# A four-layer graph network on one core: edge lists laid on 128 partitions instead of 125, and two products split into 12-bit parts

## The chip, the core and the metric

The program runs on one core of a Trainium2 chip. The core has five engines that follow their own instruction streams and wait for each other by semaphores: TensorE (PE, with its weight loads shown as PEld), VectorE (DVE), ScalarE (ACT), GpSimd (POOL) and SyncE (SP). SP, ACT and POOL also issue DMAs, each from its own queue, and all DMAs are carried out by 16 DMA engines. The metric is the device time of the whole program in microseconds; smaller is better.

## The reference

There are 3125 nodes with 256 features and 53125 directed edges (25000 random ones, their reverses, and one loop per node), sorted by target node. Four layers follow each other; each adds its result to `x`.

```python
h = relu(layernorm(x))
# layer 0: message network
m   = relu(concat(h[src], h[dst], edge_attr) @ eW1 + eb1) @ eW2 + eb2
agg = segment_sum(m, dst)
x  += layernorm(h + mlp(concat(h, agg)))
# layer 1: attention over incoming edges, with a 64-entry table of relations
k   = K[src] + 0.2 * rel_w[edge_type]        # 4 heads of 64
w   = softmax over the edges of dst of (Q[dst] . k) / 8
x  += layernorm(segment_sum(w * V[src]) @ Wo + bo + h)
# layer 2: attention with one softmax over ALL edges, edges grouped by source
# layer 3: attention with self loops, then the gates of an LSTM cell
```

## The kernel before

Nodes are handled in 25 blocks of 128. The program has a `prelude`, which counts and sorts, and then `by_slots`, which does the four layers. If a flag that the prelude computes is 0, another path (`by_blocks`) runs in its place; on these inputs the flag is 1 as long as every source block's edge count lies within the bounds that the prelude checks.

**Prelude.** The list of edges is read as `EP, EC = 125, 425`: 125 partitions with 425 consecutive edges each. `dst_i` comes by SP's queue (L254), `e_src`, `e_typ` and the shifted list `nxt_i` by ACT's queue (L261, L263, L267). After `dst_i`, SP's queue carries `x` (four loads of 6 blocks at L257 and one of the last 53 nodes at L259), the weights `w1a`, the one-row bias `b1`, and 40 DMAs that fill the whole record table `ss` with a default record (L305). DVE compares the edges with 128 low and 25 high node numbers (L330, L332; `ol` and `oh` have one buffer each, so the second half of the columns waits until PE has used the first), PE sums products of these into the degrees `pdeg` (L334). PE's stream starts with two products of `b1` (L361) that stand ahead of the first `pdeg`. Between the halves stand layer norms of `x` and the first rows of the table `a_d` of layer 0's source values. From the degrees come ranks, a scatter of the nodes in order of degree, and gathers of each node's edges into slots (`t.st`). From running sums over source blocks comes `row2`, the row of `ss` that each edge's record goes to.

**The scatter of records.** Layer 2 needs the edges grouped by source. So during layers 0 and 1 each column of the edge list is scattered to `ss`: `scatter_src(1)` issues one indirect DMA on POOL (`Kit.scatter`, L158) with one record of 66 floats from each partition, 425 in all. The records stand in `rec` tiles of `CH = 5` columns, two buffers; `loaded` reads 64 edge features per record by SP's queue (L588), one chunk ahead, and `filled` writes the two index columns by two DVE copies (L592, L593).

**Layer 0.** Work goes over 226 pairs of slots. For each pair POOL issues two gathers of 512 values (`gt`, ring of 5 pairs), and from the 19th pair on one record scatter. PE forms `ph` by two products of 128 rows (L924): the stationary operand `st` holds on one half of its rows the transposed edge features and on the other half an identity, the moving operand `wm` holds on the one half the edge rows of `eW1` and on the other half the block's own node values. DVE adds `gt` (L938) and sums the positive parts into `acc` (L941, L943). A `Clock` with ticks places the other work of a block between the pairs: `front` (node values into `wm`, two ACT copies at L715), `turned` (features into `st`, two ACT copies of 64 partitions at L733, L734), `back`, `group` and `node`. When the pairs are done, ticks go on until the last nodes are through, one record scatter at each tick; the last scatters of `kv` rows (`s_l_kv`) stand behind these on POOL, and layer 1's gathers behind them.

**Layer 1.** For each unit of up to 4 slots SP loads the slots' relation numbers, broadcast over 64 partitions (`tb`, two buffers, L980), ACT makes a one-hot of it (L985, L986), PE multiplies it by the relations (L990), POOL gathers `kv` rows (ring of 10 units), DVE forms scores (L992 on). `weighed` takes the softmax of a finished block while the next one is scored; it frees the `kv` buffers by DVE products and PE sums (L1032). `nodes` makes the rows for layer 2 (`s_l_rows`). The remaining record scatters are spread evenly over the units; the last 8 come at the end.

**Layers 2 and 3** are not touched.

The order of instructions on each engine's queue is made by a scheduler at build time, which places an instruction where its own model finds it ready. It is not the order of the source text.

Of the kernel before, what the change touches and what calls it, by code (L numbers as in the profile page):

```python
# [18 lines left out]
P = 128  # L19
# [31 lines left out]
assert sum(TILES) == NT  # L51
XH = 516
# [171 lines left out]
class Lists:  # L224


    def __init__(self, pool):
# [9 lines left out]
        self.row2 = pool.tile([EP, EC], I32, name="row2")  # L237
        self.dst_e = pool.tile([EP, EC], F32, name="dst_e")
        self.srcl_e = pool.tile([EP, EC], F32, name="srcl_e")
# [3 lines left out]
def prelude(ctx, tc, a, a_d, nodes_d, ss, st_d, flag, t):  # L243
# [9 lines left out]
    dst_i = c.tile([EP, EC], I32, name="dst_i")  # L253
    nc.sync.dma_start(dst_i, a["dst"].rearrange("(p c) -> p c", c=EC))  # L254
# [5 lines left out]
    e_src = c.tile([EP, EC], I32, name="e_src")  # L260
    nc.scalar.dma_start(e_src, a["src"].rearrange("(p c) -> p c", c=EC))  # L261
    e_typ = c.tile([EP, EC], I32, name="e_typ")
    nc.scalar.dma_start(e_typ, a["edge_type_64"].rearrange("(p c) -> p c", c=EC))  # L263
    nxt_i = c.tile([EP, EC], I32, name="nxt_i")
    nc.gpsimd.memset(nxt_i, N)
    for p0, p1, w in ((0, EP - 1, EC), (EP - 1, EP, EC - 1)):
        nc.scalar.dma_start(nxt_i[p0:p1, 0:w],  # L267
                            bass.AP(tensor=a["dst"].tensor, offset=a["dst"].offset + p0 * EC + 1,
                                    ap=[[EC, p1 - p0], [1, w]]))
# [6 lines left out]
    sfill = c.tile([P, 11, SREC], F32, name="sfill")  # L276
# [12 lines left out]
    nc.gpsimd.memset(cap[:, NB - 1:NB], float(P * TILES[NB - 1]))  # L289
    none = c.tile([1, 512], F32, name="none")  # L290
# [13 lines left out]
    for i in range(40):  # L304
        nc.sync.dma_start(ss[i * 11 * P:(i + 1) * 11 * P, :].rearrange("(p r) c -> p (r c)", p=P),  # L305
                          sfill.rearrange("p r c -> p (r c)"))

    both_e = c.tile([EP, EC, 2], I32, name="both_e")
    nc.gpsimd.tensor_copy(both_e[:, :, 0], e_src)
    nc.gpsimd.tensor_copy(both_e[:, :, 1], e_typ)  # L310
    nc.scalar.dma_start(st_d.rearrange("(p c) -> p c", c=2 * EC), both_e.rearrange("p c i -> p (c i)"))


    lo_i = wk.tile([EP, EC], I32, name="lo_i", tag="edge", bufs=4)
    nc.vector.tensor_scalar(lo_i, dst_i, 127, None, op0=ALU.bitwise_and)
    lo = c.tile([EP, EC], BF, name="lo")
    nc.vector.tensor_copy(lo, lo_i)
    hi_i = wk.tile([EP, EC], I32, name="hi_i", tag="edge", bufs=4)
    nc.vector.tensor_scalar(hi_i, dst_i, 7, None, op0=ALU.logical_shift_right)
    hi = c.tile([EP, EC], BF, name="hi")  # L320
    nc.vector.tensor_copy(hi, hi_i)
    pdeg = ps.tile([P, NB], F32, name="pdeg")
    CW = 214

    def counted(hp, c0, c1):
        w = c1 - c0
        ol = hp.tile([EP, P, CW], BF, name="ol")
        oh = hp.tile([EP, NB, CW], BF, name="oh")
        for v in range(P):
            nc.vector.tensor_scalar(ol[:, v, 0:w], lo[:, c0:c1], float(v), None, op0=ALU.is_equal)  # L330
        for v in range(NB):
            nc.vector.tensor_scalar(oh[:, v, 0:w], hi[:, c0:c1], float(v), None, op0=ALU.is_equal)  # L332
        for i in range(w):
            nc.tensor.matmul(pdeg, ol[:, :, i], oh[:, :, i], start=(c0 + i == 0), stop=(c0 + i == EC - 1))  # L334
# [33 lines left out]
    with tc.tile_pool(name="ph", bufs=1) as hp:  # L368
        counted(hp, 0, CW)
        stats()  # L370
        table(0, 5)
        counted(hp, CW, EC)
# [73 lines left out]
    sl_i = wk.tile([EP, EC], I32, name="sl_i", tag="edge", bufs=4)  # L446
    nc.vector.tensor_scalar(sl_i, e_src, 127, None, op0=ALU.bitwise_and)
    nc.vector.tensor_copy(t.srcl_e, sl_i)
    hs_i = wk.tile([EP, EC], I32, name="hs_i", tag="edge", bufs=4)
    nc.vector.tensor_scalar(hs_i, e_src, 7, None, op0=ALU.logical_shift_right)  # L450
    hs = c.tile([EP, EC], BF, name="hs")
    nc.vector.tensor_copy(hs, hs_i)
    eq = op.tile([EP, NB, EC], BF, name="eq")
# [3 lines left out]
    zero = ps.tile([EP, EC], F32, name="zero")  # L457
    nc.vector.memset(zero, 0.0)
    cum = op.tile([EP, NB, EC], F32, name="cum")
# [8 lines left out]
    tots = c.tile([EP, NB], F32, name="tots")  # L468
    nc.vector.tensor_copy(tots, cum[:, :, EC - 1])
    pc3 = ps.tile([P, 4, NB], F32, name="pc3")  # L470
    pc2, pv = pc3[:, 0:2, :], pc3[0:1, 2, :]
    nc.tensor.matmul(pc2[:EP, 0, :], k.tri[:EP, :EP], tots, start=True, stop=True)
    nc.tensor.matmul(pc2[:, 1, :], k.ones[:EP, :], tots, start=True, stop=True)
    viol = wk.tile([EP, EC], F32, name="viol", tag="edge", bufs=4)
    nc.vector.tensor_tensor(viol, dst_i, nxt_i, ALU.is_gt)
    v1 = c.tile([EP, 1], F32, name="v1")
# [5 lines left out]
    nc.vector.tensor_tensor(over, pc2[:, 1, :], cap, ALU.is_gt)  # L482
    v3 = c.tile([P, 1], F32, name="v3")
    nc.vector.tensor_reduce(v3, over, AX.X, ALU.add)
    nc.tensor.matmul(pv[:, 0:1], v1, k.ones[:EP, 0:1], start=True, stop=False)
# [5 lines left out]
    bases = c.tile([EP, NB], F32, name="bases")  # L491
    nc.vector.tensor_scalar(bases, pc2[:EP, 0, :], -1.0, None, op0=ALU.add)
# [4 lines left out]
    for b in range(NB - 1, -1, -1):  # L497
        k.gather(t.st[:, b, 0:SLOTS[b], :].rearrange("p s i -> p (s i)"), flat(st_d, 2 * E), t.off_i[:, b:b + 1], axis=1)
# [46 lines left out]
    pos_i = wk.tile([EP, EC], I32, name="pos_i", tag="edge", bufs=4)  # L545
    nc.vector.tensor_copy(pos_i, cum[:, 0])
    pa_i = wk.tile([EP, EC], I32, name="pa_i", tag="edge", bufs=4)
    nc.vector.tensor_scalar(pa_i, pos_i, 127, None, op0=ALU.bitwise_and)
    pj_i = wk.tile([EP, EC], I32, name="pj_i", tag="edge", bufs=4)
    nc.vector.tensor_scalar(pj_i, pos_i, 7, None, op0=ALU.logical_shift_right)  # L550
    step = wk.tile([EP, EC], F32, name="step", tag="edge", bufs=4)
# [3 lines left out]
    nc.vector.scalar_tensor_tensor(t.row2, hs, float(P * TM), step, op0=ALU.mult, op1=ALU.add)  # L555
    nc.vector.tensor_scalar(t.dst_e, dst_i, float(KVQ), None, op0=ALU.mult)
# [3 lines left out]
def by_slots(ctx, tc, a, out, a_d, nodes_d, ss, t):  # L560
# [19 lines left out]
    attr = a["edge_attr_64"].rearrange("(p c) k -> p c k", c=EC)  # L580
    CH = 5
    recs = ctx.enter_context(tc.tile_pool(name="s_recs", bufs=2))
    done = [0]

    def loaded(c):

        rec = recs.tile([EP, CH, SREC], F32, name="rec")
        nc.sync.dma_start(rec[:, :, 0:64], attr[:, c:c + CH, :])  # L588
        return rec

    def filled(c, rec):
        nc.vector.tensor_copy(rec[:, :, 64], dst_e[:, c:c + CH])  # L592
        nc.vector.tensor_copy(rec[:, :, 65], srcl_e[:, c:c + CH])  # L593

    rec_of = {}

    def scatter_src(n):

        for _ in range(n):
            c = done[0]  # L600
            if c == EC:
                return
            c0 = c - c % CH
            if c == 0:
                rec_of[0] = loaded(0)
                filled(0, rec_of[0])
            if c % CH == 1 and c0 + CH < EC:
                rec_of[c0 + CH] = loaded(c0 + CH)
            if c % CH == 3 and c0 + CH < EC:
                filled(c0 + CH, rec_of[c0 + CH])  # L610
            k.scatter(ss, row2[:, c:c + 1], rec_of[c0][:, c % CH, :], "src_records")
# [5 lines left out]
    with tc.tile_pool(name="s_e0", bufs=2) as wk, tc.tile_pool(name="s_e0w", bufs=1) as w, \  # L617
# [4 lines left out]
        wm = [[w.tile([P, 512], F32, name=f"wm{i}{r}") for r in range(ring)] for i in range(2)]  # L622
        st = [[w.tile([P, 4, P], F32, name=f"st{i}{r}") for r in range(ring)] for i in range(2)]
        for i in range(2):
            lo = 64 * i
            at_ = 64 - lo
            for r in range(ring):
                nc.sync.dma_start(wm[i][r][at_:at_ + 64, :], a["L0_gnn_eW1"][2 * D:2 * D + 64, :])
                for q in range(4):
                    for h in range(2):  # L630
                        nc.scalar.copy(st[i][r][lo:lo + 64, q, h * 64:h * 64 + 64],
                                       ident[lo:lo + 64, lo:lo + 64])
        both = w.tile([P, 64], F32, name="both")
        for h in range(2):
            nc.scalar.copy(both[64 * h:64 * h + 64, :], ident[64 * h:64 * h + 64, 64 * h:64 * h + 64])
        w2 = k.load_w(w, a["L0_gnn_eW2"], "w2")
# [50 lines left out]
        def front(b):  # L687
# [24 lines left out]
            yield 1  # L712
            ms[b] = [wm[h][place[b] % ring] for h in range(2)]
# [1672 lines left out]
```

## Time and profile before

| what | value |
|---|---|
| median of 15 runs | 3773.26 us (3767.17 to 3785.41) |
| profiled execution, its own time | 3777.45 us |
| span of the profile | 3775.3 us |
| busy: PE, DVE, ACT, POOL | 2346.1, 2380.1, 1096.8, 2483.4 us |
| record scatters on POOL | 425, 513.4 us busy, 1208 ns mean |
| prelude | 0 to 235 us |
| layer 0, pairs | 235 to 1254 us |
| layer 0, last nodes | 1254 to 1386 us |
| layer 1 | 1386 to 2345 us |
| layer 2 | 2345 to 3060 us |
| layer 3 | 3060 to 3776 us |

The stages are read from the first and last instructions of their tiles. A line of the profile names an engine, a source line, an operation, the tiles out<-in, partitions x elements, and a count. "Idle before <- X" is the time in which the engine stood still ahead of that instruction, and what ended it; "issue" is a gap for which the profile shows no cause.

### The profile page before, as it was taken

To read this page: it belongs to the slowest core of one execution; us is meant where nothing else is said; L and a number is where in the kernel's file an instruction comes from. 1 tells how busy PE (TensorE), PEld (TensorE's weight loads), DVE (VectorE), ACT (ScalarE), POOL (GpSimd) and SP (SyncE) were. 2 spreads that over 40 slices of the span, in tenths; PEclk is the share of its full clock that TensorE was granted. 3 is DMA by queue.
4 is the path that set the end of the run, shared out by engine and by line. 5 is a ranking of instruction groups with operands and counts; after the bars stand their busy time and mean duration, and the time that the engine had idled before them with its cause. 6 is when DMAs were issued, how large, how long until landed. Compare 5 with 4: busy or idle time off the path is not lost. (4 is left out here: it accounts for less than half of the span.)

```text
span 3775.3 us, 32562 instructions
## 1 busy us (share of the span) xinstructions
PE 2346.1 (62%) x9174; PEld 1474.8 (39%) x9174; DVE 2380.1 (63%) x4836; ACT 1096.8 (29%) x2296; POOL 2483.4 (66%) x2497
## 2 busy tenths in 40 slices
PE   5827878788877654556656665898988950112223
PEld 3313434344343334445444543566666640001111
DVE  5646566576666326667767765798988953444444
ACT  1112122222221112122322221566666630112222
POOL 3447677777777736767767654676766617667774
PEclk9858889998898756667767767899999975555556
DMA  6346465666665346656666654666666623333342
GB/s 225 128 123 175 134 182 162 171 174 172 182 169 172 83 128 169 173 162 192 188 173 193 172 155 157 199 202 204 203 208 196 192 93 106 100 97 106 109 112 71
DMA packets 295839, 595.89 MB, mean 158 GB/s; under 512 B 113501, under 2 KB 154508, under 8 KB 295650
## 3 DMA queue, kind: packets, MB, share of 16 engines
q0 software_dynamic: 163616, 472.86, 43.3%
q1 hardware_dynamic: 131512, 119.79, 10.7%
q8 instruction: 76, 1.25, 0.1%
q10 hardware_dynamic: 522, 1.06, 0.1%
q14 instruction: 113, 0.93, 0.1%
HBM read 510.85 MB, written 82.21 MB: 157 GB/s over the span
## 5 line engine op out<-in xcount | busy, mean ns | idle before, releaser
L158 POOL DMA_INDIRECT s_src_records<-rec,row x425 | 513.4, 1208 | 131.2 <-issue 119.7
L154 POOL DMA_INDIRECT kv<-s_l_rows,dst x440 | 456.3, 1037 | 217.9 <-issue 75.6
L924 PE MATMUL ph<-wm,st 128*128 128x512 f32 x904 | 474.2, 653 | 130.9 <-DVE acc L943 65.3
L154 POOL DMA_INDIRECT gt<-s_l_src,srcb x452 | 433.9, 960 | 178.1 <-issue 108.2
L154 POOL DMA_INDIRECT kv<-s_l_kv,st x439 | 420.6, 958 | 182.0 <-issue 109.2
L154 POOL DMA_INDIRECT xg<-s_l_rows,src x439 | 416.2, 948 | 133.7 <-issue 133.4
L990 PE MATMUL pk<-rel,toh 64*128 64x64 f32 x878 | 179.0, 364 | 309.1 <-DVE mk L992 179.1
L938 DVE TENSOR_TENSOR ph<-gt,ph 128x1024 f32<-128x1024 f32 x226 | 277.1, 1226 | 110.7 <-PE ph L924 98.9
L134 PE MATMUL pt<-ident,hb 128*128 128x128 f32 x50 | 16.9, 441 | 513.3 <-ACT hb L1436 513.3
L924 PEld LDWEIGHTS ph<-wm,st 128*128 128x128 f32 x904 | 178.4, 208 | 334.1 <-issue 292.3
L990 PEld LDWEIGHTS pk<-rel,toh 64*128 64x128 f32 x878 | 159.8, 268 | 342.7 <-issue 245.7
L1032 PE MATMUL acc<-kv,ident 128*128 128x256 f32 x878 | 241.0, 442 | 41.5 <-DVE kv L1028 41.5
L592 DVE COPY rec<-dst_e 125x5 f32<-125x5 f32 x85 | 17.5, 205 | 380.2 <-DMA s_src_records<-rec,row 350.7
L1287 PE MATMUL pg<-kv,oh 128*128 128x256 f32 x880 | 249.8, 409 | 3.7 <-DVE kv L1284 3.4
L985 ACT ACTIVATE toh<-tb,negp 64x512 f32<-64x512 f32 (+3 forms) x119 | 81.8, 687 | 576.2 <-PE pk L990 496.7
L943 DVE SCALAR_TENSOR_TENSOR acc<-ph,acc 128x1024 f32<-128x1024 f32 x201 | 245.0, 1219 | 3.0
L1032 PEld LDWEIGHTS acc<-kv,ident 128*128 128x128 f32 x878 | 196.2, 227 | 79.2 <-DVE kv L1028 44.8
L1472 DVE TENSOR_SCALAR sc<-xg,own 128x4 f32<-128x4 f32 (+3 forms) x119 | 31.1, 261 | 309.9 <-DMA xg<-s_l_rows,src 309.7
L134 PEld LDWEIGHTS pt<-ident,hb 128*128 128x128 f32 x50 | 7.3, 203 | 541.7 <-ACT hb L1436 540.8
L1429 DVE SCALAR_TENSOR_TENSOR acc<-xg,sc,acc 128x256 f32<-128x256 f32 x439 | 211.6, 490 | 5.3
L1242 PE MATMUL pk<-we,eat 64*128 64x256 f32 x880 | 163.7, 446 | 48.3 <-DVE mk L1248 46.8
L1248 DVE TENSOR_TENSOR mk<-kv,pk 128x512 f32<-128x512 f32 x220 | 149.6, 680 | 51.4 <-DMA kv<-s_l_rows,dst 41.3
(373 smaller groups left out, 5399.7 us busy)
## 6 DMA issues: line engine op xcount, KB each, us to landing
s_src_records<-sfill SPq DMA_DIRECT2D x40, 363.0 KB
srec<-s_src_records SPq DMA_DIRECT2D x24, 594.0 KB
rec<-in_edge_attr_dram SPq DMA_DIRECT2D x85, 156.2 KB
tb<-s_slot_types SPq DMA_DIRECT2D x101, 128.0 KB
gt<-s_l_src,srcb POOLq DMA_INDIRECT x452, 3.6
kv<-s_l_rows,dst POOLq DMA_INDIRECT x440, 3.9
kv<-s_l_kv,st POOLq DMA_INDIRECT x439, 4.0
xg<-s_l_rows,src POOLq DMA_INDIRECT x439, 2.8
```

The lines of the kernel that those rows point to most:

```text
L154: self.queued(lambda: self.nc.gpsimd.indirect_dma_start(out=to, out_offset=None, in_=table, in_offset=bass.IndirectOffsetOnAxis(ap=index, ...
L158: st = self.queued(lambda: self.nc.gpsimd.indirect_dma_start(out=table, out_offset=bass.IndirectOffsetOnAxis(ap=index, axis=0), in_=rows, ...
L924: nc.tensor.matmul(ph[:, h, :], stat[h][:, s % 4, :], ms[b][h], start=True, stop=True)
L938: nc.vector.tensor_add(ph, gt, ph)
L943: nc.vector.scalar_tensor_tensor(accs[b], ph, 0.0, accs[b], op0=ALU.max, op1=ALU.add)
L985: nc.scalar.activation(to, tb[:, 0:n * P], AF.Abs, bias=negp[:64])
L990: nc.tensor.matmul(pk[:, q, :], toh[:, q, :], rel, start=True, stop=True)
L1032: nc.tensor.matmul(acc, ident, v[:, q, :], start=(s0 + q == 0), stop=(s0 + q == C - 1))
L1242: nc.tensor.matmul(pk[:, i, :], eat[i * 64:(i + 1) * 64, q, :], we[i * 64:(i + 1) * 64, :], start=True, stop=True)
L1248: nc.vector.tensor_add(mk, o.kv[j // 2][:, :, 0:D], pk)
L1287: nc.tensor.matmul(pg, oh[:, j % T6 + i, :], v[:, i, :], start=(j + i == 0), stop=(j + i == n - 1))
L1429: nc.vector.scalar_tensor_tensor(acc, xgs[q // U3][:, q % U3, 0:D], s[:, q:q + 1], acc, op0=ALU.mult, op1=ALU.add)
```

## The change

The edge list is laid on 128 partitions with `ECW = 416` edges each. 127 partitions are full; the last one has `EL = 293` edges and is padded. Each of the four lists is loaded by a DMA over 127 rows, one for the rest, and one for the padding. Padded edges get rows behind the end of `ss`. There are 416 record scatters of 128 records. Only the last 3 record positions of each partition and block of `ss` are filled with defaults, by 3 DMAs, and the flag also asks that the other positions all get a record.

The `rec` tiles become three fixed tiles of `CH = 4` columns, loaded two chunks ahead. A chunk's columns up to 292 are loaded for 128 partitions, those from 293 on for 127.

In layer 0 the edge features fill all 128 rows of `st` (one ACT copy); `ph` is a product over one half of the rows by `w1c` for each of the two slots, in plain 32 bits, plus a product over 128 rows of a fixed 0/1 matrix `spread` by `wm` in the rounded 32-bit format (`float32r`). `wm` holds the node values in two parts: the value with its lowest 12 bits cleared (`top`, by DVE), and the remainder (by DVE).

In layer 1 the relations are split in the same way, stacked on 128 rows in `float32r`; `tb` and the one-hot `toh` cover 128 partitions.

```diff
+ECW = 416
+EL = E - (P - 1) * ECW
+FULL = (15,) * (NB - 1) + (5,)
...
+    none_i = c.tile([1, 3, ECW], I32, name="none_i")
+    for i, v in enumerate((32 * P, 0, 64 * P)):
+        nc.gpsimd.memset(none_i[:, i, :], v)
+    def edges(engine, to, of, i):
+        engine.dma_start(to[0:P - 1, :], of[0:(P - 1) * ECW].rearrange("(p c) -> p c", c=ECW))
+        engine.dma_start(to[P - 1:P, 0:EL], of[(P - 1) * ECW:E].rearrange("(p c) -> p c", p=1))
+        engine.dma_start(to[P - 1:P, EL:ECW], none_i[:, i, EL:ECW])
-    nc.sync.dma_start(dst_i, a["dst"].rearrange("(p c) -> p c", c=EC))
+    edges(nc.sync, dst_i, a["dst"], 0)
-    nc.scalar.dma_start(e_src, a["src"].rearrange("(p c) -> p c", c=EC))
+    edges(nc.scalar, e_src, a["src"], 0)
+    edges(nc.scalar, e_typ, a["edge_type_64"], 1)
...
-    for i in range(40):
-        nc.sync.dma_start(ss[i * 11 * P:(i + 1) * 11 * P, :].rearrange("(p r) c -> p (r c)", p=P),
-                          sfill.rearrange("p r c -> p (r c)"))
+    for b0, b1_ in ((0, 12), (12, NB - 1), (NB - 1, NB)):
+        n = TILES[b0]
+        r0 = b0 * P * TM
+        nc.sync.dma_start(ss[r0:r0 + (b1_ - b0) * P * n, :].rearrange("(b p j) c -> p b (j c)", p=P, j=n)
+                          [:, :, FULL[b0] * SREC:n * SREC],
+                          sfill.rearrange("p r c -> p (r c)")[:, None, :].to_broadcast([P, b1_ - b0, 3 * SREC]))
-    CW = 214
+    CW = 208
...
+    nc.vector.tensor_tensor(low, low, pc2[:, 1, :], ALU.is_gt)
+    nc.vector.tensor_add(over, over, low)
...
+    nc.sync.dma_start(t.row2[P - 1:P, EL:ECW], past)
...
-    CH = 5
-    recs = ctx.enter_context(tc.tile_pool(name="s_recs", bufs=2))
+    CH = 4
+    recs = ctx.enter_context(tc.tile_pool(name="s_recs", bufs=1))
+    ring_ = [recs.tile([P, CH, SREC], F32, name=f"rec{i}") for i in range(3)]
     def loaded(c):
-        rec = recs.tile([EP, CH, SREC], F32, name="rec")
-        nc.sync.dma_start(rec[:, :, 0:64], attr[:, c:c + CH, :])
+        rec = ring_[c // CH % 3]
+        full = min(CH, max(0, EL - c))
+        for p, w0, w1 in ((P, 0, full), (P - 1, full, CH)):
+            if w1 > w0:
+                nc.sync.dma_start(rec[0:p, w0:w1, 0:64],
+                                  bass.AP(tensor=attr.tensor, offset=attr.offset + (c + w0) * 64,
+                                          ap=[[ECW * 64, p], [64, w1 - w0], [1, 64]]))
-            if c % CH == 1 and c0 + CH < EC:
-                rec_of[c0 + CH] = loaded(c0 + CH)
+            if c % CH == 1 and c0 + 2 * CH < ECW:
+                loaded(c0 + 2 * CH)
...
+            top = wk.tile([P, 512], F32, name="top", bufs=1)
+            nc.vector.tensor_scalar(top.bitcast(I32), pb.bitcast(I32), -4096, None, op0=ALU.bitwise_and)
             for h in range(2):
-                nc.scalar.copy(ms[b][h][64 * h:64 * h + 64, :], pb[64 * h:64 * h + 64, :])
+                nc.scalar.copy(ms[b][h][0:64, :], top[64 * h:64 * h + 64, :])
+                nc.vector.tensor_sub(ms[b][h][64:P, :], pb[64 * h:64 * h + 64, :], top[64 * h:64 * h + 64, :])
...
-            nc.scalar.copy(stats[b, s][0][64:P, 0:n4, :], pt[64:P, 0:n4, :])
-            nc.scalar.copy(stats[b, s][1][0:64, 0:n4, :], pt[0:64, 0:n4, :])
+            nc.scalar.copy(stats[b, s][:, 0:n4, :], pt[:, 0:n4, :])
...
             for h in range(2):
-                nc.tensor.matmul(ph[:, h, :], stat[h][:, s % 4, :], ms[b][h], start=True, stop=True)
+                r = slice(64 - 64 * h, P - 64 * h)
+                nc.tensor.matmul(ph[:, h, :], stat[r, s % 4, :], w1c[r, :], start=True, stop=False)
+            for h in range(2):
+                nc.tensor.matmul(ph[:, h, :], spread_, ms[b][h], start=False, stop=True)
...
-            tb = wk.tile([64, U * P], F32, name="tb")
+            tb = wk.tile([P, U * P], F32, name="tb")
             nc.sync.dma_start(tb[:, 0:n * P], bass.AP(tensor=t_d.tensor, offset=t_d.offset + (b * SM + s0) * P,
-                                                      ap=[[0, 64], [1, n * P]]))
-            toh = wk.tile([64, U, P], F32, name="toh")
+                                                      ap=[[0, P], [1, n * P]]))
+            toh = wk.tile([P, U, P], FR, name="toh")
```

## The prediction

> **What bounds the kernel now.** I read the busy time by stage first, then POOL's instructions in the two stages that change, then the forms of one POOL line, then the waits, then the first 45 us. Over the span no engine looks full: POOL 66%, DVE 63%, PE 62%. In layer 0's pairs it is different.
>
> ```profile
> 1251.14 0.97 POOL L154 DMA_INDIRECT gt<-s_l_src,srcb  x1 [0.30 <-issue]
> 1252.41 0.94 POOL L154 DMA_INDIRECT gt<-s_l_src,srcb  x1 [0.30 <-issue]
> 1253.66 1.21 POOL L158 DMA_INDIRECT s_src_records<-rec,row  x1 [0.30 <-issue]
> 1255.18 1.20 POOL L158 DMA_INDIRECT s_src_records<-rec,row  x1 [0.30 <-issue]
> 1256.68 1.18 POOL L158 DMA_INDIRECT s_src_records<-rec,row  x1 [0.30 <-issue]
> ```
>
> Every indirect DMA costs its duration plus 0.30 us of issue, back to back: from 275 to 1335 us POOL's gaps beyond 0.30 sum to about 25 us. POOL is the bound there. In layer 1 (1386 to 2345) its DMAs with their 0.30 make 834 of 959 us.
>
> The forms of line 158 (min/median/max ns) carry the main reading:
>
> ```profile
> L158 POOL DMA_INDIRECT s_src_records<-rec,row x425: 1172/1210/1493, 314.9 to 2304.1; - x142
> L158 POOL DMA_INDIRECT s_l_kv<-kv,nid_i x25: 958/998/1010, 502.6 to 1382.7; - x25
> L158 POOL DMA_INDIRECT out_dram<-gg,nid_i x25: 958/985/1567, 3214.3 to 3766.6; - x25
> ```
>
> A scatter from 128 partitions takes 0.96 to 1.00 us although its rows are 1 or 2 KB; the record scatter from 125 partitions takes 1.21 with 264 bytes a row; the 1567 ns is the last block's output with 53 partitions. So the number of partitions sets it, not the bytes.
>
> The waits show the coupling of the record ring, by engine and, last, for SP's queue:
>
> ```profile
> DVE rec L592 <- DMA s_src_records<-rec,row: 350.7, 57, 12.5
> POOL kv L154 <- PE acc L1032: 53.3, 26, 13.4
> POOL s_l_rows L158 <- DVE row L1092: 49.8, 7, 21.9
> SPq L588 <- DMA s_src_records<-rec,row: 952.0, 130, 23.0
> ```
>
> DVE and SP stand behind record scatters, mostly under cover of POOL's own stream; the two POOL lines are what comes back to POOL.
>
> The start is a chain of latencies (timelines of DVE and PE):
>
> ```profile
> 7.85 0.38 DVE L315 TENSOR_SCALAR lo_i<-dst_i 125x425 int32<-125x425 int32 x1 [6.28 <-DMA dst_i<-in_dst_dram]
> 25.19 3.75 PE L361 MATMUL pa<-b,ones 1*128 1x512 f32 x4 [25.19 <-DMA b<-in_L_gnn_eb_dram]
> 28.87 15.89 PE L334 MATMUL pdeg<-oh,ol 125*128 125x25 bf16 x214
> ```
>
> PE's first half of the degrees starts right after the products of the bias, which waited for its load; DVE's second half waits for PE at 44.8.
>
> **The change part by part.**
>
> *Prelude loads.* The trace's packets: `dst_i` moves as 125 packets of 1700 bytes from 2.5 to 7.0 us, five streams of 25, each stream with a packet every 176 ns, because ACT's three lists (374 packets, done at 14.9) use the same DMA engines and take turns, 88 ns each. The last `x` load, 53 rows, runs strictly one after the other, 46 to 54 ns a packet: one engine. 125 = 5 x 25 gave five, 53 is prime and gave one; 127 is prime. I take one engine, from the 53-row load. Then `dst_i` needs 127 x 0.176 = 22.4 us and lands at 24.9, 18 later. Behind it in SP's ring on that engine stand 192 `x` packets (51 ns) and the 53, each paired with one of ACT's remaining 254 (88 ns): 192 x 0.139 + 53 x 0.136 = 33.9; then 16 of `w1a` at 84 ns, 1.3; then the bias, at 2.5 + 22.4 + 33.9 + 1.3 = 60 us, plus half a microsecond. The same sum with the old counts (25, 81 of ACT, 192, 53, 16) gives 25.1; the row says 25.19. So PE's first `pdeg` starts 35 us later, and everything that waits for it. 208 columns instead of 214 take 3% off DVE's counting and PE's products: -1. The 40 fills (issued 18.8 to 72.0) become 3; the `a_d` writes behind them on SP gain a microsecond. Prelude: +34. Bounds: -2, if 127 rows spread like 125, to +45.
>
> The Trainium skill (DMA: Bandwidth & Descriptors, on why a DMA increments its semaphore by 16) states this as a rule: the largest number up to 16 that divides the slowest dimension is the number of engines, and 127 partitions give 1. It speaks against the change, and agrees with the 125 and 53 rows.
>
> *Start of layer 0.* Three POOL memsets of `rec` are new ahead of the gathers, and `top` lengthens the first block's chain (one DVE pass of 128x512 at 0.69); 32 ACT copies (4.8 us, off the path) go. +1.
>
> *Layer 0, pairs.* PE had two 32-bit products per pair, 4 records of 0.427 us at full clock, 1.7 us. Two half-row products run at once: layer 2's pair of 64-row products (L1242, 256 columns, 4 records) is followed by the next product 0.63 us after its start, and rounded products of 256 columns follow each other every 0.12. So 512 columns: 1.0 to 1.2 for the halves, 0.45 for two rounded ones. PE is no slower, and has 20% idle in this stage; the 4.04 us of POOL per pair hide it. DVE gains per block `top` and two subtractions of 64x512, at 0.69 each by the 128x512 row: 2.1 x 25 = 52 us on 629 of 1019; ACT loses copies. Both stay under POOL. If that cover went, DVE's 52 us would show.
>
> The skill (TensorEngine Tiling, Key Properties) says that a change of tiling mode drains the array. The row above has the drain in its 0.63; two such drains a pair would cost at most some 0.3 us of PE's slack.
>
> POOL: the scatter follows a gather, 1.21 now, 0.99 then (the `out` row, likewise between gathers). 208 x 0.22 = -46. Bounds: 0.26 each (-54) and none.
>
> *Layer 0, last nodes.* 52 scatters back to back go from 1.18 to 0.96: -11. DVE's copies into `rec` stand between the node work in its queue and wait for scatters. In the built order the last such copy still needs the 260th scatter, in both kernels; but after it the changed queue has one more node's work, from its normalisation to the next node's sum: before, that stood between the copies at 1311.4 and 1336.9; its bare rows (6 for the norm and row, 2 + 3.8 for the two products, about 5 for DVE behind them) make 17 us. +17, bounds 0 and +25.
>
> *Layer 1.* 165 scatters x 1.51 = 249 become 156 x 1.29 = 201: -48. What of it arrives depends on POOL's 119 us of gaps here: 48 from `acc` (kv buffers held), 74 from `row`. Two things move them. DVE's `rec` copies stand less far ahead of the gathers than before in the built order: I take 15 off the first. Against this, SP's queue: the loads of `tb` stand behind `rec` loads that wait for scatters. Before, the next `tb` belonged to a unit whose gathers came about 23 POOL DMAs after the awaited scatter; now about 6, some later than that. And from column 293 on a `rec` load has 127 rows of four 256-byte packets. The old load is 625 such packets, 18 ns each, never more than five at once, 2.2 us undisturbed and 3.4 typical here. 508 on one engine: 508 x 18 = 9.1, times 3.4/2.2 = 14 us, and `tb`'s share on that engine waits behind. With the scatter's landing (1.3 + 3.2) and the load's start, `tb` comes about 21 us after the awaited scatter, needed about 14 after it: 7 us late on average for 31 of the units, up to 20. The kv ring gives blocks of 5 units about 4 units (30 us) of slack, so POOL is mostly covered; the `row` scatters are not. I take +30 for both kinds of gap. The broadcast on 128 rows doubles 128 KB loads: 15 MB of 596. Layer 1: -48 - 15 + 30 = -33. Bounds: -70 (gaps fall too) to +70 (the 31 late units each pass about 4 of their 7 us on).
>
> *Layers 2 and 3*: not touched, 0.
>
> **Sum.** +34 + 1 - 46 - 11 + 17 - 33 = -38 on the profiled execution's 3777.45 us (span 3775.3, 2.15 around it): 3739. The median of the runs is 4.2 lower, so 3735.
>
> **Rivals.**
> *A, the late `tb` rules layer 1 (slower).* For: 31 one-engine loads in a stage where SP already waits 952 us behind scatters, and `tb` with two buffers only. Against: before, ACT waited for `tb` 11 times and 79.5 us without POOL standing still. The point from which it decides: the sum without the +30 is -68, so 68/31 = 2.2 us of stall per load. With 4 us, 31 x 4 = 124, it ends at 3735 - 30 + 124 = 3829; just past the point, 3785.
> *B, 127 rows spread over several engines.* For: a DMA may be cut differently than its rows suggest. Against: the 53-row load. Then the prelude and layer 1's late loads cost nothing: 3735 - 34 - 30 = 3671; with the prelude's part alone 3701.
> *C, the scatter does not get cheaper at 128 rows.* For: no 264-byte scatter of 128 rows is in the trace. Against: three scatters of 128 rows at 1.00 with larger rows, and `at` gathers at 0.95. Then 9 scatters x 1.5 remain of the gain: 34 + 1 + 17 - 13 + 15 = +54, 3827.
> *D, gains and losses meet.* The layer 1 gain goes into gaps while the prelude loses 34: 3735 + 33 = 3768.
> That the flag falls to 0, and `by_blocks` runs, is excluded: the inputs' source blocks hold 2089 to 2233 edges, the last 881, against bounds of 1920 to 2304 and 640 to 1024.
>
> **How the numbers follow.** A change under 0.2%, 7.5 us, can't be told from none. Chances: forecast 0.54 (own range 3705 to 3764), B 0.13, D 0.13, A 0.17, C 0.03. Faster takes the forecast, B and some of D: 0.70; same 0.10; slower takes A, C: 0.20. The range reaches down into B and up past A's near end: 3682 to 3795.
>
> **What would show it.** Right: record scatters at 0.96 to 1.00; `lo_i` near 25 us and the first `pdeg` near 64; the first gather of layer 0 about 34 us later than 235; layer 0's last gather about 12 us earlier than 1253. Layer 1's length near 926. Wrong: `lo_i` near 8 us (B), scatters at 1.2 (C), ACT waiting for `tb` for hundreds of us together with POOL gaps at `kv` (A).

## The result: 3798 us, slower by 0.6%

The changed kernel takes 3798.34 us (median of 10 runs, 3790.36 to 3809.25), the kernel before 3775.05 us beside it (50 runs). The ratio is 1.0062, with a 95% interval of 1.0051 to 1.0072. The forecast was 3735 us in a range of 3682 to 3795: the sign was wrong, and the time lies 3 us above the range.

The table is read from POOL's instructions in the two profiled executions, which took 3777.45 and 3804.18 us. A stage runs from its first to its last gather or scatter, layer 0's pairs from the first gather of `gt` (the 235 us named ahead as the prelude's end is the first gather of edge features, `at`, 5 us earlier); "gaps" is POOL's idle time beyond the 0.30 us that each DMA costs to issue.

| us | before | changed | difference | forecast |
|---|---|---|---|---|
| first gather of layer 0 | 240.7 | 277.2 | +36.5 | +34 + 1 |
| layer 0, pairs (gaps) | 1012.7 (45) | 987.7 (60) | -25.0 | -46 |
| layer 0, last nodes | 133.1 | 124.8 | -8.3 | -11 + 17 |
| layer 1 (gaps) | 952.8 (119) | 966.7 (178) | +13.9 | -33 |
| layers 2 and 3 | 1428.9 | 1435.0 | +6.1 | 0 |

The differences add up to 23.2 us, as much as the medians differ by; the two profiled executions differ by 26.7. The other 3.5 lie behind the last output scatter, where one last instruction of POOL's, a drain, takes 4.5 us instead of 1.3.

The record scatter became as cheap as foreseen. This is the line's form in the changed kernel, then in the kernel that the experiments end with (columns: count, then min/median/max in ns):

```profile
L162 POOL DMA_INDIRECT s_src_records<-rec,row x416: 963/1005/1282, 353.9 to 2317.5; - x139
```

```profile
L162 POOL DMA_INDIRECT s_src_records<-rec,row x416: 963/1005/1217, 317.0 to 2220.0; - x139
```

1.21 us became 1.00, and 416 x 0.21 with nine scatters less is about 100 us of POOL's stream. So the question is where these 100 us went. The start is the easy part: timelines of DVE and PE in the changed kernel.

```profile
21.34 0.38 DVE L337 TENSOR_SCALAR lo_i<-dst_i 128x416 int32<-128x416 int32 x1 [19.79 <-DMA dst_i<-none_i]
52.25 3.75 PE L383 MATMUL pa<-b,ones 1*128 1x512 f32 x4 [52.25 <-DMA b<-in_L_gnn_eb_dram]
55.93 16.84 PE L356 MATMUL pdeg<-oh,ol 128*128 128x25 bf16 x208
```

`dst_i` came 13.5 us later than before and the bias 27 us later, and with it PE's first half of the degrees.

Layer 1 is the surprise. Three lines of the waits of the kernel before, then five of the changed kernel (in all us, times, longest):

```profile
ACT toh L985 <- DMA tb<-s_slot_types: 79.5, 11, 24.2
POOL gt L154 <- DVE ph L938: 46.0, 23, 19.4
DVE yg L1068 <- DMA xw<-s_x: 10.5, 4, 5.5
```

```profile
ACT toh L1030 <- DMA tb<-s_slot_types: 202.6, 28, 19.1
POOL kv L158 <- PE acc L1077: 69.6, 23, 19.2
POOL gt L158 <- DVE ph L975: 61.8, 30, 18.6
POOL s_l_rows L162 <- DVE row L1137: 59.9, 8, 31.5
DVE yg L1113 <- DMA xw<-s_x: 46.7, 5, 14.0
```

ACT stands 203 us for `tb` where it stood 80, and DVE 47 us for `xw` where it stood 10.5. What both have in common is SP's queue. A stretch of it in layer 1, changed kernel (start, duration of the issue itself, what is issued), and DVE in the same stretch:

```profile
2089.72 0.26 SPq L619 DMA_DIRECT2D rec<-in_edge_attr_dram  x1
2090.07 9.05 SPq L1025 DMA_DIRECT2D tb<-s_slot_types  x1
2099.18 5.60 SPq L1111 DMA_DIRECT2D xw<-s_x  x3
2110.05 0.26 SPq L619 DMA_DIRECT2D rec<-in_edge_attr_dram  x1
2110.41 10.69 SPq L1049 DMA_DIRECT2D vb<-s_l_v  x1
```

```profile
2088.95 0.93 DVE L1073 TENSOR_TENSOR kv<-kv,wt 128x768 f32<-128x768 f32 x1
2103.88 0.55 DVE L1113 SCALAR_TENSOR_TENSOR yg<-yg,rs,xw 128x256 f32<-128x256 f32 x1 [14.00 <-DMA xw<-s_x]
```

The DMA that is issued right after a record load of 127 rows takes SP 9 to 11 us to issue here, not 0.3. Until then nothing else goes out: `xw` was issued 9 us late, and DVE did nothing for 14 us. Over layer 1, issues of SP that took more than 2 us number 3 with 7 us in sum before, and 29 with 242 us in the changed kernel. Each of the 29 follows directly on such a record load; they take 3.7 to 11.1 us, 8.6 in the median. The packets agree: such a load's 508 packets of 256 bytes take 10.6 us in the median (7.3 to 14.5) with never more than two recorded at a time; the 512 packets of a 128-row load take 1.3 us. What makes an issue stop is not shown. It is not the sign of a 127-row load alone: at the start of the kernel before, two issues behind loads of `x` take 5.3 and 5.5 us.

### The profile page after: what moved, and what is told of

Read it like the earlier page. It is cut to its first block, busy times and chain, and to the rows that moved or that the text cites. A ratio compares the mean times of both kernels' runs of the same rounds, so it can differ in the third digit from the quotient of the medians.

```text
span 3802.1 us, 32573 instructions
## 1 busy us (share of the span) xinstructions
PE 2242.8 (59%) x9178; PEld 1368.9 (36%) x9178; DVE 2428.5 (64%) x4954; ACT 1059.1 (28%) x2201; POOL 2391.3 (63%) x2496
## 5 line engine op out<-in xcount | busy, mean ns | idle before, releaser
L162 POOL DMA_INDIRECT s_src_records<-rec,row x416 | 417.2, 1003 | 127.3 <-issue 117.0
L959 PE MATMUL ph<-w1c,st 64*128 64x512 f32 x904 | 283.5, 692 | 108.7 <-DVE acc L980 89.6
L1035 PE MATMUL pk<-rel,toh 128*128 128x64 f32 x439 | 103.3, 363 | 358.9 <-DVE mk L1037 216.9
L1030 ACT ACTIVATE toh<-tb,negp 128x512 fp32r<-128x512 f32 (+3 forms) x119 | 81.8, 687 | 564.4 <-PE pk L1035 354.4
L1035 PEld LDWEIGHTS pk<-rel,toh 128*128 128x128 f32 x439 | 89.1, 271 | 375.7 <-issue 247.8
L625 DVE COPY rec<-dst_e 128x4 f32<-128x4 f32 x104 | 18.7, 182 | 313.4 <-DMA s_src_records<-rec,row 297.1
L1037 DVE TENSOR_TENSOR mk<-kv,pk 128x1024 f32<-128x1024 f32 (+3 forms) x119 | 136.7, 1148 | 69.1 <-DMA kv<-s_l_kv,st 64.2
```

The source lines that it names most:

```text
L162: st = self.queued(lambda: self.nc.gpsimd.indirect_dma_start(out=table, out_offset=bass.IndirectOffsetOnAxis(ap=index, axis=0), in_=rows, ...
L959: nc.tensor.matmul(ph[:, h, :], stat[r, s % 4, :], w1c[r, :], start=True, stop=False)
L1035: nc.tensor.matmul(pk[:, q, :], toh[:, q, :], rel, start=True, stop=True)
L1037: nc.vector.tensor_tensor(mk[:, 0:n].rearrange("p s (h d) -> p s h d", h=4), kv[:, 0:n, 0:D].rearrange("p s (h d) -> p s h d", h=4), pk[:, ...
```

## The experiments

Each edit is shown against the changed kernel. Every ratio is to the kernel before on the same chip. On three of the chips (runs e1 to e6, r3, d1 and d2) the kernel before took 4188 to 4255 us, and all kernels stand in waits that are absent elsewhere. These runs are told last, though most of them came first: e1 to e6 and r3 ahead of r2, and d1 and d2 ahead of m1 and m2. The readings rest on runs on two other chips, on which the kernel before took 3776 to 3779 us.

**The record loads (r2).** The 127-row loads become one of 112 and one of 15 rows.

```diff
-        for p, w0, w1 in ((P, 0, full), (P - 1, full, CH)):
+        for p0, p, w0, w1 in ((0, P, 0, full), (0, 112, full, CH), (112, P - 1, full, CH)):
```

> The changed kernel with only the record loads split in 112 and 15 rows, once more beside the kernel before. Theory (the one-engine record loads block SP's queue): of SP's DMA issues in layer 1 none or one takes over 2 us where the changed kernel has 29 with 242 us; layer 1 shrinks from 966 to 915 to 925 us; a ratio of 0.991 to 0.996 where the changed kernel has 1.006. Rival (DVE's and PE's chain holds layer 1): SP's issues are short all the same and layer 1 stays at 955 to 970, ratio 1.003 to 1.007.

Measured: 3747.97 us, ratio 0.9925 (0.9903 to 0.9947). Layer 1 takes 913.6 us, 53 less than in the changed kernel; its other stages are the same within 3 us. No issue of SP in layer 1 takes more than 2 us, and the 508 packets take 2.3 us in the median. The waits of this kernel, and its `tb` issues (third number: the longest, in ns) after those of the changed kernel:

```profile
ACT toh L1030 <- PE pk L1035: 435.9, 89, 22.0
ACT toh L1030 <- DMA tb<-s_slot_types: 65.8, 11, 14.0
```

```profile
L1025 SPq DMA_DIRECT2D tb<-s_slot_types x119: 319/327/11107, 1396.1 to 2256.0; - x119
```

```profile
L1025 SPq DMA_DIRECT2D tb<-s_slot_types x119: 319/320/1787, 1391.4 to 2200.8; - x119
```

So the loads of 127 rows cost layer 1 53 us, and without them it is 39 us shorter than before. The rival that DVE and PE hold layer 1 falls. How much of the 53 us is the stopped issues, and how much the packets of `tb` that may wait behind the record load's, no run separates: the split takes both away.

**Both splits (n3).** The lists of the prelude too, as 112 and 15 rows.

```diff
-        engine.dma_start(to[0:P - 1, :], of[0:(P - 1) * ECW].rearrange("(p c) -> p c", c=ECW))
+        for p0, p1 in ((0, 112), (112, P - 1)):
+            engine.dma_start(to[p0:p1, :], of[p0 * ECW:p1 * ECW].rearrange("(p c) -> p c", c=ECW))
...
-    for p0, p1, w in ((0, P - 1, ECW), (P - 1, P, EL - 1)):
+    for p0, p1, w in ((0, 112, ECW), (112, P - 1, ECW), (P - 1, P, EL - 1)):
```

> Both splits (edge lists and record loads as 112 and 15 rows), everything else as changed. Theory: the two gains add, 50 us from the records and 30 to 35 from the start: first gather of layer 0 at 240 to 246 us, layer 1 905 to 920 us, 3712 to 3722 us, a ratio of 0.982 to 0.986. Rival (the earlier start is lost again in layer 0, whose order changes): ratio 0.990 to 0.993.

Measured: 3718.92 us, ratio 0.9863 (0.9831 to 0.9895). The first gather of layer 0 comes at 246.1 us, 29 us earlier than with the record loads alone; layer 1 takes 912.6. The two gains add. That the first gather is still 5.4 us later than before, though the degrees are ready 0.9 us sooner, is in good part the new POOL work ahead of it: from POOL's last small preparations to the first gather of features pass 5.0 us in the changed kernel, with three memsets of `rec` in between, and 1.2 before.

**The new products, taken out one by one (n7, n8, n6).** All three have both splits. n7 has layer 0's products as before, n8 layer 1's relations as before, n6 both: the layout alone.

```diff
-                nc.tensor.matmul(ph[:, h, :], stat[r, s % 4, :], w1c[r, :], start=True, stop=False)
-            for h in range(2):
-                nc.tensor.matmul(ph[:, h, :], spread_, ms[b][h], start=False, stop=True)
+                nc.tensor.matmul(ph[:, h, :], stat[h][:, s % 4, :], ms[b][h], start=True, stop=True)
...
-            tb = wk.tile([P, U * P], F32, name="tb")
+            tb = wk.tile([64, U * P], F32, name="tb")
```

> Both splits, and layer 0's products with their operands and copies as before; layer 1 as changed. Theory (the 12-bit parts on DVE open the new POOL gaps of layer 0's pairs): the pairs' stage falls from about 987 to 968 to 975 us, 10 to 20 us faster than both splits alone. Rival (the gaps come from the cheaper scatters, which leave less cover): the stage stays at 983 to 990 us and the time is the same within 6 us.

> Both splits, and layer 1's relations as before (64 rows of tb, four-pass products, 76 us more of PE); layer 0 as changed. Theory (PE's products are under cover, and half of tb's bytes are saved): layer 1 within 10 us of both splits alone, to either side. Rival (with cheaper scatters PE's chain of one-hot, product and scores is what POOL's buffers wait for): layer 1 20 to 60 us longer.

> The layout on 128 partitions alone: both splits, products of layers 0 and 1 as before. Theory: scatters at 1.00 us and no slow loads: prelude as before, layer 0's pairs 965 to 975 us, layer 1 905 to 930 us, 3695 to 3725 us. Rival (POOL's saved time turns into waits in layer 1 without the new products): layer 1 935 to 970 us, 3740 to 3775 us.

Measured beside n3 on the same chip:

| kernel | time, us | ratio to before | layer 0 pairs (gaps) | layer 1 |
|---|---|---|---|---|
| n3, all new products | 3718.92 | 0.9863 (0.9831 to 0.9895) | 985.1 (59) | 912.6 |
| n8, layer 0's only | 3723.67 | 0.9867 (0.9836 to 0.9899) | 983.3 (53) | 919.0 |
| n7, layer 1's only | 3708.53 | 0.9828 (0.9797 to 0.9859) | 968.0 (39) | 915.0 |
| n6, none | 3700.27 | 0.9807 (0.9776 to 0.9837) | 971.6 (45) | 913.7 |

The four runs of n6 (3696.75 to 3706.85) and of n3 (3712.22 to 3723.41) do not overlap. Layer 0's products cost 12 to 17 us of the pairs' stage, in both pairs of kernels that differ in them alone (n8 against n6, n3 against n7). Layer 1's relations show no gain: with and without them the stage differs by 6 us one way and 1 us the other. The layout alone, with loads that are cut well, beats both kernels: 75 us less than the kernel before, 98 less than the changed one.

**What of layer 0's products costs it (m1, m2).** m1 keeps PE's new products and lets ACT copy the node values in one rounded part (their low bits are left out). m2 is n6 with the same three DVE passes per block added, whose results nobody reads. Each also moves one tick: the pass that makes `top` has a tick of its own in `front`, which m1 loses and m2 gains. The second edit is shown against n6.

```diff
-            top = wk.tile([P, 512], F32, name="top", bufs=1)
-            nc.vector.tensor_scalar(top.bitcast(I32), pb.bitcast(I32), -4096, None, op0=ALU.bitwise_and)
-            yield 1
...
-                nc.scalar.copy(ms[b][h][0:64, :], top[64 * h:64 * h + 64, :])
-                nc.vector.tensor_sub(ms[b][h][64:P, :], pb[64 * h:64 * h + 64, :], top[64 * h:64 * h + 64, :])
+                nc.scalar.copy(ms[b][h][0:64, :], pb[64 * h:64 * h + 64, :])
```

```diff
+            top = wk.tile([P, 512], F32, name="top", bufs=1)
+            nc.vector.tensor_scalar(top.bitcast(I32), pb.bitcast(I32), -4096, None, op0=ALU.bitwise_and)
+            yield 1
...
                 nc.scalar.copy(ms[b][h][64 * h:64 * h + 64, :], pb[64 * h:64 * h + 64, :])
+                nc.vector.tensor_sub(top[64 * h:64 * h + 64, :], pb[64 * h:64 * h + 64, :], top[64 * h:64 * h + 64, :])
```

> Both splits and the new products of layer 0 without DVE's parts (the low bits of the node values are left out). Theory (DVE's three passes per block are the cost): the pairs' stage 968 to 973 us. Rival (PE's products or their place in PE's order are the cost): 982 to 988 us.

> The layout alone with the old products and the same three DVE passes per block added, whose results nobody reads. Theory (DVE's passes are the cost): the pairs' stage 983 to 988 us. Rival: 968 to 975 us.

The pairs' stage of n6, m2 and m1, in this order (the stage, its length, then busy time of PE, PEld, DVE, ACT and POOL, the granted clock, DMA share, GB/s):

```profile
244.80:1216.40 971.60, 793.80 (x2347) 399.69 (x2348) 628.33 (x904) 216.03 (x439) 710.10 (x725) 0.91 0.61 178
```

```profile
246.10:1232.60 986.50, 801.04 (x2340) 402.14 (x2341) 674.73 (x978) 215.26 (x439) 709.99 (x725) 0.91 0.60 175
```

```profile
246.20:1225.40 979.20, 794.73 (x2787) 379.14 (x2789) 630.76 (x904) 181.89 (x375) 710.94 (x725) 0.89 0.60 176
```

With old products and 46 us more of DVE's work (m2) the stage is 986.5 us, as long as with the new products (985.1, n3). But it is not the same wait that makes it so. These are the waits of POOL that differ, of n6, of n3, of m1 and, the last two, of m2:

```profile
POOL gt L158 <- DVE ph L971: 44.8, 31, 17.1
```

```profile
POOL gt L158 <- DVE ph L976: 59.8, 28, 18.7
```

```profile
POOL gt L158 <- DVE ph L977: 55.8, 35, 15.8
```

```profile
POOL gt L158 <- DVE ph L975: 44.9, 22, 19.3
POOL s_src_records L162 <- DVE rec L627: 17.2, 5, 10.9
```

In m2 the added time stands ahead of record scatters that wait for DVE's copies into `rec`: 17.2 us, where n6 has one such wait of 3.7 us in this stage and n3 none worth naming. In n3 and m1 it stands where gathers wait for DVE to be done with `ph`. So m2 shows that this much DVE work can cost 15 us, though DVE is busy 68% of the stage and POOL's stream is the same; that its length is that of n3 is chance, and it does not show that the passes are the cost in the changed kernel. There m1 is the nearer test: without the passes the stage is 979.2, between the two expected values, 6 us below n3 and 8 to 11 above n6 and n7, and the longer wait for `ph` stays. So PE's new products are not a gain either. How the 12 to 17 us divide between the passes, the products and the order that the scheduler makes anew for each kernel stays open: n6 and n7, alike in layer 0, differ by 4 us. The times were 3714.77 (m1) and 3720.91 us (m2), two runs each, beside 3779.40 for the kernel before on that chip.

**The runs where the kernel before took 4188 to 4255 us.** e1 is the prelude's split alone, e2 the same kernel as r2, e3 and r3 as n3, e6 as n6; e4 and e5 are the changed kernel, with its 127-row loads, with layer 0's products or layer 1's relations as before; d1 and d2 are the kernels of m1 and m2.

> The changed kernel with each list's 127-row load cut into 112 and 15 rows (the four edge lists of the prelude; nothing else). Theory (127 rows go through one DMA engine and hold up the bias behind them): lo_i moves from 21.3 us back to 6 to 10, the product of the bias from 52.25 to 22 to 28, the first gather of layer 0 from 277 to 242 to 248; the time falls from 3798 by about 33, to 3765. Rival (the later start comes from the new arithmetic and the extra small loads, not from the rows of one load): lo_i may move but the first gather stays within 5 us of 277, time 3793 to 3800.

> The changed kernel with the record loads from column 293 on cut into 112 and 15 rows (nothing else). Theory (late relation numbers behind one-engine loads are what layer 1 lost): ACT's wait for tb falls from 203 us to about 80, POOL's gaps in layer 1 from 147 us to about 95, layer 1 from 966 us to 915 to 925; time about 3798 - 45 = 3753. Rival (layer 1 is now held by DVE's and PE's chain, and the cheaper scatters only became gaps): tb's wait may fall, but layer 1 stays 955 to 970 us, time 3790 to 3800. Second rival (tb doubled is the load that matters): tb's wait stays above 150 us, time 3785 to 3800.

> The changed kernel with layer 0's products, their operands and copies as before (no half-row products, no 12-bit parts, the ACT copies back); 128 partitions, and layer 1 as changed. Theory (the 14 us of new POOL gaps in layer 0's pairs come from DVE's parts of the node values and their later arrival): the pairs' stage falls from 987 to about 970 us; the time to about 3783. Rival (PE's new products set these gaps): the same fall, but ph's wait for PE falls and not DVE's busy time. Rival (DVE's parts cost nothing, gaps come from the order): 985 to 990, time 3796 to 3800.

> The changed kernel with layer 1's relations as before: 64 rows of tb, a 32-bit one-hot and relations, PE's four-pass products back (439 products, 179 us of PE's time where the parts take 103). Theory of the one-engine record loads: layer 1 stays 955 to 975 us, tb's wait for ACT 150 to 210, time 3790 to 3805. Rival (the doubled tb is what comes late): tb's wait falls to about 80 us, layer 1 to 915 to 930, time about 3755.

> The changed kernel with both splits: the edge lists' and the record loads' 127 rows as 112 and 15. Theory (one-engine loads cost the start 33 us and layer 1 some 45): first gather of layer 0 at 242 to 248 us, ACT's wait for tb about 80 us, time 0.979 to 0.985 of the kernel before where the changed kernel has 1.006. Rival (layer 1's loss is not the record loads): the start's part alone, a ratio of 0.996 to 0.999, and tb's wait stays above 150 us.

> The layout of 128 partitions alone: both splits, and the products of layer 0 and of layer 1 in the form that they had before. Theory: scatters at 1.00 us save 85 us of POOL's stream; layer 0's pairs 965 to 972 us (POOL gaps there back at about 42), layer 1 905 to 930 us; ratio to the kernel before 0.975 to 0.985. Rival (POOL's saved time turns into waits for PE and DVE in layer 1): layer 1 stays at 945 to 970 us, ratio 0.990 to 1.000. Rival (the parts in layer 1 are a gain that layer 1 needs once the scatters are cheaper): the ratio is above that of the kernel with both splits and the new products.

> The changed kernel with both splits once more, since the earlier comparison was made where the kernel before took 4255 us and stood in waits that its profile at 3775 us does not have. Theory: a ratio of 0.979 to 0.985, first gather of layer 0 at 242 to 248 us, layer 1 915 to 930 us. Rival (layer 1's loss is not the record loads): 0.996 to 0.999, layer 1 955 to 970 us.

> Both splits and the new products of layer 0, without DVE's parts: ACT copies the block's node values into the rounded operand in one part and the second part is zero throughout, so the low bits of the node values are left out. Theory (DVE's three passes per block, 52 us, are the cost): the pairs' stage 968 to 973 us, DVE's busy time in it about 628 us. Rival (PE's products or their place in PE's order are the cost): the stage stays at 982 to 988 us with DVE at 628.

> The layout alone (both splits, old products in layers 0 and 1), with the same three DVE passes per block added, whose results nobody reads: the masking pass and two subtractions. Theory (DVE's passes are the cost): the pairs' stage rises from 972 to 983 to 988 us and the time from 3700 to 3711 to 3718. Rival (the passes fit beside POOL's stream, and the cost came from the operand waiting for them or from PE): the stage stays at 968 to 975 us and the time within 6 us of 3700.

| kernel | ratio to before | first gather | layer 0 pairs (gaps) | layer 1 (gaps) |
|---|---|---|---|---|
| e1 | 0.9996 (0.9968 to 1.0025) | 244.8 | 1132 (207) | 1115 (326) |
| e2 | 1.0057 (1.0026 to 1.0088) | 275.6 | 1123 (197) | 1105 (317) |
| e4 | 1.0054 (1.0018 to 1.0090) | 275.4 | 1115 (186) | 1131 (342) |
| e5 | 1.0196 (1.0140 to 1.0253) | 278.9 | 1120 (195) | 1176 (388) |
| e3 | 0.9966 (0.9936 to 0.9997) | 247.8 | 1126 (196) | 1119 (327) |
| r3 (as e3) | 0.9957 (0.9929 to 0.9985) | 246.2 | 1144 (219) | 1127 (338) |
| e6 | 1.0085 (1.0048 to 1.0123) | 251.0 | 1133 (205) | 1208 (419) |
| d1 | 0.9945 (0.9904 to 0.9986) | 246.7 | 1129 (199) | 1131 (339) |
| d2 | 1.0258 (1.0202 to 1.0315) | 251.3 | 1181 (250) | 1190 (399) |

The scatter is at 1.00 us there too, and the first gather moves by the same 31 us (e1 against e2): the prelude's part is confirmed on its own. The bias's product starts at 20.66 us in e1. Nearly all else drowns in new gaps, 186 to 250 us in the pairs' stage where n3 has 59. (The 147 us of gaps that the expectation of e2 starts from are 178 by the count used here.) In layer 1 of e2 they look like this:

```profile
1591.62 0.72 ACT L1030 ACTIVATE toh<-tb,negp 128x512 fp32r<-128x512 f32 x1 [9.03 <-remote]
1591.62 1.23 DVE L1037 TENSOR_TENSOR mk<-kv,pk 128x1024 f32<-128x1024 f32 x1 [6.74 <-remote]
1602.82 0.72 ACT L1030 ACTIVATE toh<-tb,negp 128x512 fp32r<-128x512 f32 x1 [9.72 <-remote]
1602.82 1.23 DVE L1037 TENSOR_TENSOR mk<-kv,pk 128x1024 f32<-128x1024 f32 x1 [7.45 <-remote]
```

ACT and DVE, which wait for different loads, go on at the same instant, and the profile knows no releaser of the program ("remote"); the last packets of `tb` had ended 6.5 us before. What delays these arrivals wasn't found. There the verdict on layer 1's products turns round: the three kernels with the old relations (e5, e6, d2) take 1176 to 1208 us in layer 1, the six with the new ones (e1 to e4, r3, d1) 1105 to 1131, and the layout alone is slower than the kernel before. Both splits with the new products (n3; e3, r3) are faster than it on both chips on which they ran, on this one by 0.4%.

## Why the prediction was wrong, step by step

*Right: the bound and the scatter.* POOL's stream sets layer 0's pairs; 207 scatters there fell by 42 us (forecast 46 for 208), and the 128-partition rows of other lines were the right price. Rival C falls.

*Right: the start, its sum in part by luck.* One engine for 127 rows was taken from the 53-row load; forecast +34 and +1, measured +36.5, and -29 to -31 when the loads are split. Within it the sizes were off and made up for each other: the bias was forecast at 60.5 and came at 52.25, so the degrees came 29.2 us later, not 34; and another 7.3 us, not 1, lie between them and the first gather, 3.8 of them in POOL's memsets. Rival B falls. The rule of the Trainium skill (DMA: Bandwidth & Descriptors, on why a DMA increments its semaphore by 16), that the largest divisor up to 16 of the slowest dimension is the number of engines, agrees with both edits: 127 rows ran with never more than two packets at a time, and the same bytes as 112 and 15 rows went out four to five times as fast.

*Wrong, the largest step: layer 1, "I take +30 for both kinds of gap" and the 15 us taken off.* The place was right (record loads of 127 rows ahead of `tb` in SP's queue) and so, roughly, was the load's length (forecast 14 us, measured 10.6). Two things were missed. The loads cost 53 us, 1.8 us for each of 30, not 30. I had the load wait in one engine's queue and `tb`'s share behind it; the trace shows that the issue itself stops, so that SP stands for 4 to 11 us and every later load with it, `xw`, `vb` and `hb` too: 242 us of issues, in which DVE waits as well. And the 15 us that I took off the gaps for earlier `rec` copies did not come: without the slow loads (r2) POOL's gaps in layer 1 are 124 us against 119 before, and the stage is 39 us shorter where the forecast without the +30 is 63. So of the 47 us by which layer 1 was missed, 23 are the loads and 24 the gain that did not arrive. This is the mechanism of rival A, at a price below the 2.2 us per load from which it would have decided alone. With the loads at the 30 us of the forecast the change would have come out about even (23 less 23, an estimate), so the sign took the other steps too. Rival D, in which gains and losses meet at 3768, had the right kind and not the size.

*Wrong: layer 0's pairs, "both stay under POOL".* DVE's 52 us were costed at nothing because DVE was idle for 38% of the stage, and PE's products because PE was idle for 20%. Together they cost 12 to 17 us (n8 against n6, n3 against n7). Average idle time is no cover for work that stands ahead of what POOL's buffers wait for: the waits of `gt` for DVE's `ph` went from 46 to 62 us, with thirteen between 1 and 5 us where there had been none of that size. Leaving DVE's passes out gives 6 us back (m1); which part of the rest is PE's products and which the new order isn't shown. PE's products were no slower in sum: PE's busy time in the stage is 802 us with the new products (n3) and 802 with the old (n7).

*Wrong: the last nodes.* Forecast -11 and +17, measured -8.3. The scatters gave 11, and the wait of the last `kv` scatters for DVE rose from 46 to 49 us, not by 17. That one more node's work stands behind the last copies was read from the built order; its price as a serial chain did not show in the run.

*Not explained: layers 2 and 3*, +6.1 where no line was touched; layer 3 takes 676 to 678 us in every kernel with the new layout on these chips, against 672.6.

*The sum.* Forecast against measured, in the order of the table: 35 - 46 + 6 - 33 + 0 = -38, and 36.5 - 25.0 - 8.3 + 13.9 + 6.1 = +23.2. Of the 61 us between, layer 1 is 47, the pairs 21, layers 2 and 3 6 and the start 1.5; the last nodes gave 14 back. In the pairs, some 14 of the 21 are new gaps, 4 the scatters, and the rest is in POOL's `gt` gathers, whose busy time rose by 3.5 us.

## What to carry to other kernels

Padding a list to 128 partitions paid here, where an indirect DMA per column was the bound, once the loads that the padding left with 127 rows were cut into 112 and 15. Such a load can cost more than its own length, since the queue that issued it may stop issuing; look for issues that take microseconds in the timeline of the issuing engine. Judge a cause by the wait that makes it, not by the length alone: m2 is as long as n3 by another wait. And split a large change: here the layout was worth 75 us, and the arithmetic that came with it cost some 18; on one of the chips where all kernels were slower it was a gain of 55 (e3 against e6).

## What was not expected of the hardware

An issue of `tb` on SP took up to 11.1 us (0.33 in the median) when the DMA before it was a record load of 127 rows, 508 packets of which never more than two moved at a time. The records of PE for some 222 pairs take nearly the same time as two products of 128 rows in plain 32 bits (461 us, n7) and as two half-row products and two rounded ones (279 + 174 us, changed kernel). And on three chips the kernel before took 11 to 13% longer, in waits that ended for several engines at once. There the kernels with layer 1's old relations took 45 to 90 us longer in that layer than kernels with the new ones on the same chip (e5 against e4, d2 against d1, e6 against e3), which they did not elsewhere; these pairs differ in other things too.
